# Seven quarter products instead of eight in the gated products of the experts' second parts

## The chip, the core and the metric

The kernel runs on one core of a Trainium2 chip. The metric is the device time of one execution in microseconds (us): lower is better. The core has a matrix engine (TensorE, PE in the profile, with its weight loads shown apart as PEld), a vector engine (VectorE, DVE), an activation engine (ScalarE, ACT), GpSimd (POOL) and SyncE (SP), which here issues most of the loads. Matrix products write to PSUM, from where VectorE and ScalarE read them; everything else lies in SBUF. All data is 32-bit floating point. One matrix product of the kernel appears in the profile as two TensorE instructions.

## The reference, cut to what matters

Eight sequences of 256 tokens with 512 features pass through two layers. Each layer adds a recurrent attention over a context and then a feed-forward network. Layer 0's network is dense. Layer 1's is a mixture of eight experts: every token goes to two of them, and the outputs are weighted by the gate. One expert computes, with its own three matrices,

```
g = x @ w1.T          # tokens x 1024
l = x @ w3.T          # tokens x 1024
t = g * sigmoid(g) * l
y = t @ w2.T          # tokens x 512
out[token] += weight[token] * y
```

The change touches the two products `g` and `l` alone, and how the three matrices lie in SBUF.

## The kernel before

Until about 908 us the kernel runs the attention of both layers, layer 0's network and the dispatch, which writes every token's features, its index and its gate weight into its two experts' queues in DRAM, and it computes the first parts of experts 6 and 7. Then it works off the other parts. An expert's queue is computed in two **parts** (`PARTS`): the first 256 places and the following 336. The first part always runs. The second stands in a branch (`tc.If(needed > 0)`, line 736) and runs if the queue is longer than the first part. Longer queues still would be handled by `overflow` (line 865), which has a branch of its own and nothing to do in the measured data.

The order of parts is 6_1, 7_1, 0_0, 0_1, 1_0, 1_1 and so on to 5_1, where 0_1 is expert 0's second part. The loop at lines 891 to 905 issues, for each part: the load of the next expert's weights (`load_expert`, `fill_expert`, `fill_w13`), the reading of the branch's condition on TensorE, ScalarE and VectorE, and the part (`part`, `expert_part`). Beside the part runs a background generator `bg`, one step of it after each hidden chunk: `prepare` (line 652) loads the tokens of coming parts (`r`, line 671) and turns them with TensorE transposes (`turn`, lines 643 to 648; `rt` in the profile), so that features lie on partitions.

In `compute` the 1024 hidden features of an expert are eight chunks `k` of 128. `hidden` multiplies, for chunk k, the four 128x128 blocks of `w1` with the tokens into the PSUM tile `gp`, and those of `w3` into `lp`. In a first part both fit in one PSUM bank (`gl`, 2 x 256 columns). ScalarE takes the tanh of half of `gp` (line 548), VectorE multiplies it out (lines 549, 550), and `add` (line 703) accumulates `y` for two or three blocks of 128 tokens over all chunks. The y products of chunk k are issued behind the gated products of chunk k+1. PSUM has three banks for `gp`/`lp`/`gl` and three for `y`. At a part's end `weigh` (line 725) multiplies by the gate weight and adds to the old rows that `old_rows` gathered (GpSimd, line 679), and `new_rows` scatters them (line 687). In the last part, 5_1, the y products of all chunks stand at the end, block by block, so that each block can leave while the next is multiplied.

A tile scheduler sets the order of instructions on each engine and the waits; where `manual_schedule` is named, the program's own order holds for an engine. A tile pool has a fixed number of buffers, and a new tile waits for the last reader of the tile whose buffer it takes. The weights have a pool of two buffers of 48 KB per partition (`wts`); the tokens and most activations are in `v4` (11 buffers of 4 KB), and token rows, old rows and small tiles are in `u2` (16 buffers).

Of the kernel before, what the change touches and what calls it, by code (L numbers as in the profile page):

```python
# [17 lines left out]
P = 128  # L18
# [32 lines left out]
def flamingo_kernel(  # L51
# [20 lines left out]
    nc = tc.nc  # L72

    const = ctx.enter_context(tc.tile_pool(name="const", bufs=1))
    wts = ctx.enter_context(tc.tile_pool(name="wts", bufs=2))
    work = ctx.enter_context(tc.tile_pool(name="work", bufs=2))
    small = ctx.enter_context(tc.tile_pool(name="small", bufs=2))
    dram = ctx.enter_context(tc.tile_pool(name="dram", bufs=1, space=DRAM))
# [1 line left out]
    ps_o = ctx.enter_context(tc.tile_pool(name="ps_o", bufs=3, space=PSUM))  # L80
    ps_st = ctx.enter_context(tc.tile_pool(name="ps_st", bufs=2, space=PSUM))

    def v4(name):
        return work.tile([P, DC, T], FP, tag="v4", name=name, bufs=11)

    def u2(shape, name):
        return work.tile(shape, FP, tag="u2", name=name, bufs=16)
# [25 lines left out]
    def load_first():  # L113
# [4 lines left out]
            nc.sync.dma_start(out=t[:, :, bs], in_=ctx_in[:, :, bs])  # L118
        return t

    def new_w13(name):
        return tuple(wts.tile([P, DC, HH], FP, tag=t, name=f"{t}_{name}") for t in ("w1", "w3"))

    def fill_w13(tiles, *srcs):
        for t, src in zip(tiles, srcs):
            nc.sync.dma_start(out=t, in_=src.rearrange("(c p) h -> p c h", p=P))
        return tiles

    def load_const(src, shape, name):
        t = const.tile(shape, FP, tag=name, name=name)  # L130
# [2 lines left out]

    first_ctx = load_first()

    w2h = [wts.tile([P, KC, D], FP, tag="w2", name=f"w2_{n}") for n in "ab"]
    turned = dram.tile([H0, D], FP, name="turned")

    def by_kj(ap, i):
        return ap.rearrange("(k j i) d -> i k j d", j=8, i=16)[i]  # L140

    for i in range(16):
        nc.sync.dma_start(out=w2h[i // KC][:, i % KC, :], in_=by_kj(W2T, i))
    wcol = [load_const(w0, [P, DC], "w0c"), load_const(td1, [P, DC], "w1c")]
    ucol = [load_const(u0, [P, DC], "u0c"), load_const(tf1, [P, DC], "u1c")]
    tgx = load_const(g_xattn.partition_broadcast(P), [P, 2], "tgx")
# [34 lines left out]
    nc.vector.memset(taken, 0.0)  # L181


    empty = constant([P, 1, ROW], "empty")
    nc.gpsimd.memset(empty[:, :, :D], 0.0)
    nc.gpsimd.memset(empty[:, :, D:], NOBODY)

# [200 lines left out]


    def transform(mat, i, scale):  # L390
        w = w2h[i // KC][:, i % KC, :]
        ps = ps_o.tile([P, D], FP, tag="o", name=f"fw_{i}")
        nc.tensor.matmul(ps, lhsT=mat, rhs=w, start=True, stop=True)
        nc.scalar.activation(w, ps, AF.Copy, scale=scale)

    def fwht_kj():
        for i in range(16):
            transform(hadm, i, 1.0)
            if i % 4 == 3:
                lo = i - 3  # L400
                for m in range(lo, i + 1):
                    nc.sync.dma_start(out=by_kj(turned, m), in_=w2h[m // KC][:, m % KC, :])
            yield

    latest_load = [None]

    def fwht_i():
        for h in range(2):
            latest_load[0] = nc.sync.dma_start(
                out=w2h[h], in_=turned[h * HH : (h + 1) * HH, :].rearrange("(k p) d -> p k d", p=P)  # L410
            )
        yield
        for k in range(16):
            transform(had16, k, 0.5 / H0 ** 0.5)
            yield
# [114 lines left out]
    latest = [None]  # L530

    def hidden(xn, w1, w3, k, width, name, t=None, both=None):
        cols = slice(k * P, (k + 1) * P)
        if both is not None:
            gp, lp = both[:, 0, :], both[:, 1, :]
        elif 2 * width <= 512:
            both = ps_gl.tile([P, 2, width], FP, tag="gl", name=f"gl_{name}")
            gp, lp = both[:, 0, :], both[:, 1, :]
        else:
            gp = ps_gl.tile([P, width], FP, tag="gl", name=f"gp_{name}")  # L540
            lp = ps_gl.tile([P, width], FP, tag="gl", name=f"lp_{name}")
        for ps, w in ((gp, w1), (lp, w3)):
            for c in range(DC):
                latest[0] = nc.tensor.matmul(ps, lhsT=w[:, c, cols], rhs=xn(c)[:, :width], start=(c == 0), stop=(c == DC - 1))  # L544

        if t is None:
            t = h1(width, f"t_{name}")
        nc.scalar.activation(t, gp, AF.Tanh, scale=0.5)  # L548
        nc.vector.scalar_tensor_tensor(t, t, 1.0, gp, ALU.add, ALU.mult)  # L549
        nc.vector.tensor_tensor(t, t, lp, ALU.mult)  # L550
        return t
# [51 lines left out]
    def ffn_out(s, hs, bg, n):  # L603
        for c in range(DC):
            o = ps_o.tile([P, T], FP, tag="o", name=f"o_f{s}_{c}")
            for k in range(2 * KC):
                nc.tensor.matmul(  # L607
                    o, lhsT=w2h[k // KC][:, k % KC, c * P : (c + 1) * P], rhs=hs[k],
                    start=(k == 0), stop=(k == 2 * KC - 1),
                )  # L610
                if k % 4 == 3:
                    run(bg, n)
            nc.vector.scalar_tensor_tensor(
                x[s][:, c, :], o, tgf[:, 0:1], x[s][:, c, :], ALU.mult, ALU.add
            )
# [2 lines left out]
    experts = {}  # L618

    def new_expert(name):  # L620
        return (*new_w13(name), wts.tile([P, KC, D], FP, tag="w2", name=f"w2_{name}"))

    def fill_expert(tiles, e):
        fill_w13(tiles, w1T[e], w3T[e])
        nc.sync.dma_start(out=tiles[2], in_=w2T[e].rearrange("(k p) d -> p k d", p=P))
        return tiles

    def load_expert(e):
# [18 lines left out]
        for dst, cs in dsts:  # L647
            nc.scalar.copy(dst, tp[:, cs, :rows])

    parts, metas = {}, {}  # L650

    def prepare(e, i):
        lo, width = PARTS[i]
        name = f"{e}_{i}"
        n = -(-width // P)
        mt = small.tile([P, n, 4], FP, tag="mt", name=f"mt_{name}", bufs=9)
        r0 = e * NT + lo
        nc.sync.dma_start(out=mt, in_=queue[r0 : r0 + n * P, D:ROW].rearrange("(b p) d -> p b d", p=P))
        metas[name] = unpack(e, mt, n, f"e{name}")
        per = DC if DC * width <= DC * T else 2  # L660
        tiles = [v4(f"q_{name}_{j}") for j in range(DC // per)]
        views = [
            t.rearrange("p c t -> p (c t)")[:, : per * width].rearrange("p (c t) -> p c t", c=per)
            for t in tiles
        ]
        yield
        for b in range(n):
            rows = min(P, width - b * P)
            bs = slice(b * P, b * P + rows)
            r = u2([P, D], f"r_{name}_{b}")  # L670
            nc.sync.dma_start(out=r[:rows, :], in_=queue[r0 + b * P : r0 + b * P + rows, :D])
            dsts = [(v[:, :, bs], slice(j * per, (j + 1) * per)) for j, v in enumerate(views)]
            turn(r, dsts, f"{name}_{b}", rows)
            yield
        parts[name] = lambda c: views[c // per][:, c % per, :]

    def old_rows(who, b, end, name):
        g = u2([P, D], f"g_{name}")
# [17 lines left out]
    def compute(weights, xq, wt, g, width, name, bg=iter(()), n=0, leave=None):  # L696
        w1, w3, w2 = weights
        blocks = [(b, min(P, width - b * P)) for b in range(len(g))]
        ys = [ps_o.tile([P, D], FP, tag="o", name=f"y_{name}_{b}") for b, _ in blocks]
        ts = []  # L700

        def add(k, b, rows):
            nc.tensor.matmul(  # L703
                ys[b][:rows, :], lhsT=ts[k][:, b * P : b * P + rows], rhs=w2[:, k, :],
                start=(k == 0), stop=(k == KC - 1),
            )

        for k in range(KC):
            ts.append(hidden(xq, w1, w3, k, width, f"{name}_{k}"))
            if k > 0 and leave is None:  # L710
                for block in blocks:
                    add(k - 1, *block)
            run(bg, n)
        for b, rows in blocks:
            for k in range(KC - 1 if leave is None else 0, KC):
                add(k, b, rows)
            if leave is not None:
                weigh(g[b], ys[b], wt, b, rows)
                leave(b)
        if leave is None:  # L720
            for b, rows in blocks:
                weigh(g[b], ys[b], wt, b, rows)

    def weigh(g, y, wt, b, rows):
        nc.vector.scalar_tensor_tensor(  # L725
            g[:rows, :], y[:rows, :], wt[:rows, b : b + 1], g[:rows, :], ALU.mult, ALU.add
        )

    def expert_part(weights, xq, meta, width, name, bg, n, end=NT, needed=None, last=False):
        who, wt = meta  # L730
        blocks = range(-(-width // P))
        g = [old_rows(who, b, end, f"{name}_{b}") for b in blocks]
        if needed is None:
            compute(weights, xq, wt, g, width, name, bg, n)
        else:
            with tc.If(needed > 0):  # L736
                compute(
                    weights, xq, wt, g, width, name, leave=(lambda b: new_rows(who, b, g[b], end)) if last else None
                )
        if not last:  # L740
            for b in blocks:
                new_rows(who, b, g[b], end)
# [55 lines left out]

    def part(e, i, bg, n, end=NT, needed=None, last=False):
        name = f"{e}_{i}"  # L800
        expert_part(experts[e], parts[name], metas[name], PARTS[i][1], name, bg, n, end, needed, last)

    bg = chain(wkv(1, NS - 1), dispatch(NS - 1))
    for e in EARLY:
# [86 lines left out]
    for at, (e, i) in enumerate(todo):  # L891
# [9 lines left out]
            engines = busy + [mybir.EngineType.Pool] * (at == len(todo) - 1)  # L901
            needed = nc.values_load(needs[0:1, e : e + 1], engines=engines, min_val=0, max_val=1)  # L902
        bg = prepare_on(at)
        part(e, i, bg, 1, NT, needed, at == len(todo) - 1)
        take(bg)


# [44 lines left out]
```

## Time and profile before

| | us |
|---|---|
| median of three runs | 1601.11 (1598.48 to 1602.63) |
| the profiled execution, its own time | 1602.78 |
| its span in the trace | 1601.1 |
| mean granted TensorE clock | 0.986 |
| TensorE busy, 913 to 1600 us | 664.6 of 687 |
| VectorE busy, 913 to 1600 us | 126.1 |
| ScalarE busy, 913 to 1600 us | 61.1 |
| mean DMA share, 913 to 1600 us | 0.25 |

A group line of the profile reads: line, engine, operation, output <- inputs with buffer numbers left out, size of the weight block, output shape, count | busy time and mean duration in ns | idle time ahead of it on its engine and what ended it. A timeline line reads: start, duration of the whole run of like instructions, engine, line, operation, count, and idle time before it in brackets. TensorE's instructions overlap, so the distance between two starts is the cost of one, not its duration. `gp`, `lp` are a second part's products, `gl` a first part's, `gl_f` layer 0's, `y` the output products of the experts.

One expert takes about 100.3 us of TensorE from the start of one first part (1188.63) to the next (1288.9): some 43.5 us for the first part and 56.8 for the second.

### The profile page before, as it was taken

The page shows a single profiled execution, that of the slowest core. Times are in us where ns is not written, and L with a number is a line of the kernel's source. Part 1 is how long each engine was busy: PE and PEld are TensorE (multiplying, and loading weights), DVE is VectorE, ACT ScalarE, POOL GpSimd, SP SyncE. Part 2 cuts the span into 40 slices and gives each one's busy share as a digit, 9 for nine tenths or more (in the row PEclk, how much of TensorE's full clock was granted, in tenths as well). Part 3 has the DMA queues.
Part 4 walks back from the last instruction along what each step waited for, and adds up shares of the span by engine and source line. Part 5 has one row for each costly group of instructions (what it writes and reads, how often), then busy time and mean ns, then how long its engine had stood idle before and what let it go on. Part 6 is the DMA issues. An engine that isn't in the chain of part 4 may idle for free. (4 is left out here: it accounts for less than half of the span.)

```text
span 1601.1 us, 16764 instructions
## 1 busy us (share of the span) xinstructions
PE 1524.4 (95%) x6496; PEld 1149.8 (72%) x6496; DVE 762.6 (48%) x1779; ACT 270.6 (17%) x641; POOL 143.7 (9%) x190
## 2 busy tenths in 40 slices
PE   5999999999999999999999899899999999999996
PEld 2978788787888878888787655476667576675763
DVE  6582886868788687887337212122112121121221
ACT  5140222122121221222111100011001010010100
POOL 1000001010000101001101201012101011010110
PEclk9999999999999999999999999999999999999998
DMA  9950000010100101001441305146041050420000
GB/s 350 358 177 14 27 27 27 27 54 27 38 29 14 54 14 47 21 14 72 182 181 47 95 0 189 69 151 214 30 175 56 17 219 27 172 73 13 26 30 17
DMA packets 67802, 134.97 MB, mean 84 GB/s; under 512 B 11644, under 2 KB 25084, under 8 KB 67712
## 3 DMA queue, kind: packets, MB, share of 16 engines
q1 hardware_dynamic: 57600, 108.44, 18.7%
q0 software_dynamic: 8960, 25.25, 4.5%
q8 instruction: 55, 0.90, 0.2%
q14 instruction: 35, 0.29, 0.1%
q10 hardware_dynamic: 1152, 0.09, 0.0%
HBM read 100.05 MB, written 37.90 MB: 86 GB/s over the span
## 5 line engine op out<-in xcount | busy, mean ns | idle before, releaser
L703 PE MATMUL y<-w_e,t 128*128 128x512 f32 (+1 forms) x592 | 270.4, 592 | 0.0
L544 PE MATMUL gl<-q,w_e 128*128 128x256 f32 x1024 | 236.8, 384 | 8.7 <-DVEq L868 6.8
L544 PE MATMUL gl_f<-xn,w_b 128*128 128x256 f32 (+1 forms) x1152 | 236.0, 361 | 1.6 <-DVE t_f L550 1.6
L544 PEld LDWEIGHTS gl<-q,w_e 128*128 128x128 f32 x1024 | 194.9, 193 | 52.3 <-issue 28.2
L544 PE MATMUL gl_f<-xn,w_a 128*128 128x256 f32 (+1 forms) x1152 | 230.9, 359 | 1.0 <-DVE xn L272 0.9
L544 PEld LDWEIGHTS gl_f<-xn,w_b 128*128 128x128 f32 x1152 | 202.9, 193 | 29.4 <-issue 2.6
L544 PEld LDWEIGHTS gl_f<-xn,w_a 128*128 128x128 f32 x1152 | 200.2, 193 | 24.0 <-DVE xn L272 1.2
L703 PEld LDWEIGHTS y<-w_e,t 128*128 128x128 f32 (+1 forms) x592 | 107.8, 182 | 107.5 <-issue 93.2
L544 PE MATMUL gp<-q,w_e 128*128 128x336 f32 x448 | 137.5, 451 | 2.5 <-issue 2.5
L544 PE MATMUL lp<-q,w_e 128*128 128x336 f32 x448 | 135.7, 446 | 0.0
L549 DVE SCALAR_TENSOR_TENSOR t<-t,gp 128x336 f32<-128x336 f32 x56 | 28.2, 504 | 220.9 <-ACT t L548 220.9
L549 DVE SCALAR_TENSOR_TENSOR t<-t,gl 128x256 f32<-128x256 f32 x64 | 26.7, 418 | 222.9 <-ACT t L548 222.9
L544 PEld LDWEIGHTS gp<-q,w_e 128*128 128x128 f32 x448 | 85.9, 192 | 58.5 <-issue 25.2
L607 PE MATMUL o_f<-t_f,w_b 128*128 128x256 f32 x512 | 123.5, 383 | 2.3 <-DVE t_f L550 2.3
L607 PE MATMUL o_f<-t_f,w_a 128*128 128x256 f32 x512 | 123.7, 382 | 0.0
L544 PEld LDWEIGHTS lp<-q,w_e 128*128 128x128 f32 x448 | 85.1, 190 | 41.6 <-issue 0.2
L303 DVE RECIPROCAL e<-e 128x512 f32<-128x512 f32 (+1 forms) x34 | 107.4, 3158 | 0.0
L607 PEld LDWEIGHTS o_f<-t_f,w_a 128*128 128x128 f32 x512 | 97.2, 191 | 13.4 <-issue 0.5
L607 PEld LDWEIGHTS o_f<-t_f,w_b 128*128 128x128 f32 x512 | 94.2, 190 | 15.9 <-DVE t_f L550 4.7
L548 ACT ACTIVATE t_f<-gl_f 128x256 f32<-128x256 f32 (+1 forms) x144 | 50.1, 355 | 264.8 <-PE gl_f L544 264.0
L687 POOL DMA_INDIRECT out<-g,who_e x40 | 40.3, 1006 | 595.6 <-DVE g L725 460.6
L548 ACT ACTIVATE t<-gp 128x336 f32<-128x336 f32 x56 | 25.3, 451 | 334.0 <-PE gp L544 334.0
(182 smaller groups left out, 1215.9 us busy)
## 6 DMA issues: line engine op xcount, KB each, us to landing
w_e<-in_w1T SPq DMA_DIRECT2D x8, 2048.0 KB
w_e<-in_w3T SPq DMA_DIRECT2D x8, 2048.0 KB
w_e<-in_w2T SPq DMA_DIRECT2D x8, 2048.0 KB
queue<-empty SPq DMA_DIRECT2D x8, 1290.0 KB
r<-queue SPq DMA_DIRECT2D x32, 256.0 KB
c<-in_ctxT SPq DMA_DIRECT2D x15, 512.0 KB
out<-xr SPq DMA_DIRECT2D x16, 256.0 KB
x<-in_xT SPq DMA_DIRECT2D x7, 512.0 KB
```

The costliest lines, as they stand in the source:

```text
L303: nc.vector.reciprocal(den, den)
L544: latest[0] = nc.tensor.matmul(ps, lhsT=w[:, c, cols], rhs=xn(c)[:, :width], start=(c == 0), stop=(c == DC - 1))
L548: nc.scalar.activation(t, gp, AF.Tanh, scale=0.5)
L549: nc.vector.scalar_tensor_tensor(t, t, 1.0, gp, ALU.add, ALU.mult)
L607: nc.tensor.matmul(o, lhsT=w2h[k // KC][:, k % KC, c * P : (c + 1) * P], rhs=hs[k], start=(k == 0), stop=(k == 2 * KC - 1),)
L687: nc.gpsimd.indirect_dma_start(out=out[:end, :], out_offset=bass.IndirectOffsetOnAxis(ap=who[:, b : b + 1], axis=0), in_=g, in_offset=None ...
L703: nc.tensor.matmul(ys[b][:rows, :], lhsT=ts[k][:, b * P : b * P + rows], rhs=w2[:, k, :], start=(k == 0), stop=(k == KC - 1),)
```

## The change

In a second part of 336 tokens each of the two gated products, a matrix of 1024 x 512 times one of 512 x 336, is divided once in each of its three dimensions: the weights into four quarters of 512 hidden features by 256 input features, the tokens into four quarters of 256 features by 168 tokens. Plain multiplication has eight quarter products. The changed kernel forms seven (Strassen's scheme in Winograd's form), of sums of the quarters, and combines the seven results by additions. One step `k` now gives the hidden chunks k and k+4 together, so there are four steps instead of eight.

- **Weights as quarter tiles.** `w1` and `w3` of an expert are four tiles each, `w2` is four tiles, all of 0.5 MB. Each has a transfer of its own: twelve per expert instead of three. They lie in the pool of the activations, which grows from 11 to 35 buffers of the same size; the weights' own pool is gone.
- **Sums of the weights** (`sum_weights`): for each of `w1` and `w3` three new tiles, and a fourth sum written over quarter `a21` (`last_sum`) once nothing reads `a21` any more. They are made on VectorE in the background of the expert's first part, the last ones right ahead of the second part's branch. **Sums of the tokens** (`sum_tokens`): four operations on VectorE.
- For expert 7, whose first part lies before the loop, both are issued just ahead of the branch of 6_1. For expert 6 no sums are made: 6_1 keeps `compute`.
- **`compute_paired`** replaces `compute` in the other seven second parts. In a step, for each of the two matrices: three products of two matmuls each into the tile `pa`, three into `pb`, and the seventh products of both matrices into one tile `pc`. ScalarE copies one product, VectorE adds the others in four operations and, for `pc`, one more; then follow one tanh and two VectorE operations over 672 columns. The y products of a step are issued among the products of the next (`late`, `put`). TensorE's order in it is written out by hand (`manual_schedule`).
- In a first part the background now takes two steps after each chunk instead of one. The tile `empty` moves to the pool `u2`, and the hidden tiles of second parts as well.

```diff
     def fill_w13(tiles, *srcs):
-        for t, src in zip(tiles, srcs):
-            nc.sync.dma_start(out=t, in_=src.rearrange("(c p) h -> p c h", p=P))
+        for j in range(2):
+            for t, src in zip(tiles, srcs):
+                for i in range(2):
+                    nc.sync.dma_start(
+                        out=t[i][j],
+                        in_=src[i * 2 * P : (i + 1) * 2 * P, j * D : (j + 1) * D].rearrange("(c p) h -> p c h", p=P),
+                    )
...
+    HALF = PARTS[1][1] // 2
+
+    def sum_weights(e, last=False):
+        sums[e] = []
+        for n, w in zip("13", experts[e]):
+            (a11, a21), (a12, a22) = w
+            s1, s2, s4 = (v4(f"s{i}_{n}_{e}", (P, 2, D)) for i in (1, 2, 4))
+            sums[e].append((a11, a12, a22, s1, s2, a21, s4))
+            nc.vector.tensor_tensor(s1, a21, a22, ALU.add)
+            yield
+            nc.vector.tensor_tensor(s2, s1, a11, ALU.subtract)
+            yield
+            nc.vector.tensor_tensor(s4, a12, s2, ALU.subtract)
+            yield
+        if last:
+            last_sum(e)
+
+    def last_sum(e):
+        for a11, *_, s3, _ in sums[e]:
+            nc.vector.tensor_tensor(s3, a11, s3, ALU.subtract)
+
+    def sum_tokens(name):
...
+        nc.vector.tensor_tensor(t1, b12, b11, ALU.subtract)
+        nc.vector.tensor_tensor(t2, b22, t1, ALU.subtract)
+        nc.vector.tensor_tensor(t3, b22, b12, ALU.subtract)
+        nc.vector.tensor_tensor(t4, b21, t2, ALU.subtract)
...
+        def product(ps, to, k, weights, toks):
+            for c in range(2):
+                nc.tensor.matmul(
+                    ps[:, to, :], lhsT=weights[:, c, k * P : (k + 1) * P], rhs=toks[:, c, :],
+                    start=(c == 0), stop=(c == 1),
+                )
+
+        def six(k, n):
+            a11, a12, a22, s1, s2, s3, s4 = sums[e][n]
+            r = u2([P, 4, HALF], f"h{n}_{name}_{k}")
+            ps = ps_gl.tile([P, 3, HALF], FP, tag="gl", name=f"pa{n}_{name}_{k}")
+            product(ps, 0, k, a11, b11)
+            product(ps, 1, k, a12, b21)
+            product(ps, 2, k, s2, t2)
+            nc.scalar.copy(r[:, 1, :], ps[:, 0, :])
+            nc.vector.tensor_tensor(r[:, 0:4:3, :], ps[:, 1:3, :], twice(r[:, 1:2, :]), ALU.add)
+            yield
+            ps = ps_gl.tile([P, 3, HALF], FP, tag="gl", name=f"pb{n}_{name}_{k}")
+            product(ps, 0, k, s1, t1)
+            product(ps, 1, k, s3, t3)
+            product(ps, 2, k, s4, b22)
+            nc.vector.tensor_tensor(r[:, 1:3, :], ps[:, 0:2, :], twice(r[:, 3:4, :]), ALU.add)
+            nc.vector.tensor_tensor(r[:, 3, :], ps[:, 1, :], r[:, 1, :], ALU.add)
+            nc.vector.tensor_tensor(r[:, 1, :], ps[:, 2, :], r[:, 1, :], ALU.add)
+            yield r
...
+        for k in range(KC // 2):
+            last = k == KC // 2 - 1
+            rs = []
+            for n in range(2):
+                both = six(k, n)
+                next(both)
+                put(2 * n if not last else 0)
+                rs.append(next(both))
+            put(2 if not last else 0)
+            ps = ps_gl.tile([P, 2, HALF], FP, tag="gl", name=f"pc_{name}_{k}")
+            for n in range(2):
+                product(ps, n, k, sums[e][n][2], t4)
+            put(len(late))
+            for n in range(2):
+                nc.vector.tensor_tensor(rs[n][:, 2, :], ps[:, n, :], rs[n][:, 2, :], ALU.add)
+            t = u2([P, 4, HALF], f"t_{name}_{k}")
+            nc.scalar.activation(t, rs[0], AF.Tanh, scale=0.5)
+            nc.vector.scalar_tensor_tensor(rs[0], t, 1.0, rs[0], ALU.add, ALU.mult)
+            nc.vector.tensor_tensor(rs[1], rs[0], rs[1], ALU.mult)
...
+            if leave is None:
+                late += [(j, b, rows) for j in (k, k + 4) for b, rows in blocks]
+        put(len(late))
+        for b, rows in blocks:
+            if leave is not None:
+                for i in range(KC):
+                    add(i // 2 + i % 2 * 4, b, rows)
+            weigh(g[b], ys[b], wt, b, rows)
...
     def expert_part(weights, xq, meta, width, name, bg, n, end=NT, needed=None, last=False):
...
+            paired = weights in sums
+            if paired and weights not in EARLY:
+                last_sum(weights)
...
             with tc.If(needed > 0):
-                compute(
-                    weights, xq, wt, g, width, name, leave=(lambda b: new_rows(who, b, g[b], end)) if last else None
-                )
+                if paired:
+                    with tc.manual_schedule(engines={mybir.EngineType.PE}):
+                        compute_paired(weights, sums[name], wt, g, name, done)
+                else:
+                    compute(experts[weights], xq, wt, g, width, name, leave=done)
...
         bg = prepare_on(at)
-        part(e, i, bg, 1, NT, needed, at == len(todo) - 1)
+        if i == 0:
+            bg = chain(bg, sum_tokens(f"{e}_1"), sum_weights(e))
+        elif e == EARLY[0]:
+
+            take(chain(sum_weights(EARLY[1], True), sum_tokens(f"{EARLY[1]}_1")))
+        part(e, i, bg, 2, NT, needed, at == len(todo) - 1)
         take(bg)
```

## The prediction

> **What bounds the kernel now.** I read the busy shares first, then the groups by line, then the timeline of TensorE in one expert, then the list of TensorE's waits after 913 us.
>
> ```profile
> PE 1524.4 (95%) x6496; PEld 1149.8 (72%) x6496; DVE 762.6 (48%) x1779; ACT 270.6 (17%) x641; POOL 143.7 (9%) x190
> ...
> PEclk9999999999999999999999999999999999999998
> ...
> L544 PE MATMUL gp<-q,w_e 128*128 128x336 f32 x448 | 137.5, 451 | 2.5 <-issue 2.5
> L544 PE MATMUL lp<-q,w_e 128*128 128x336 f32 x448 | 135.7, 446 | 0.0
> L549 DVE SCALAR_TENSOR_TENSOR t<-t,gp 128x336 f32<-128x336 f32 x56 | 28.2, 504 | 220.9 <-ACT t L548 220.9
> ```
>
> TensorE is busy 95% of the span at nearly full clock, and VectorE waits 220.9 us for work ahead of line 549: the bound is TensorE. The change touches the experts' second parts, the groups with 336 columns. They have 448 + 448 hardware instructions, 128 to a part, so **seven** second parts run, not eight. Which one is skipped stands in the timeline:
>
> ```profile
> 1081.04 3.60 PE L703 MATMUL y<-w_e,t 128*128 128x512 f32 x8
> 1086.53 8.83 PE L544 MATMUL gl<-q,w_e 128*128 128x256 f32 x32 [1.89 <-DVEq L736]
> ...
> 1128.43 3.60 PE L703 MATMUL y<-w_e,t 128*128 128x512 f32 x8
> 1131.87 2.42 PE L544 MATMUL gp<-q,w_e 128*128 128x336 f32 x8
> 1134.13 2.42 PE L544 MATMUL lp<-q,w_e 128*128 128x336 f32 x8
> 1136.39 2.42 PE L544 MATMUL gp<-q,w_e 128*128 128x336 f32 x8
> 1138.65 2.42 PE L544 MATMUL lp<-q,w_e 128*128 128x336 f32 x8
> 1140.91 2.74 PE L703 MATMUL y<-w_e,t 128*128 128x512 f32 x6
> ```
>
> Expert 0's first part ends at 1084.6 and expert 1's first part (`gl`) follows at once, with no `gp` between: 0_1 does not run. Part 6_1 keeps the old form. So six parts are paired at run time: 7_1, 1_1, 2_1, 3_1, 4_1, 5_1. Starts 2.26 us apart for 8 instructions give a **pitch** of 282.5 ns per 336-column instruction (the mean of 446 to 451 counts overlapping ends).
>
> **The gain on TensorE.** A second part has 8 chunks x 2 matrices x 4 matmuls x 2 instructions = 128, at 282.5 ns: 36.16 us. After, 4 steps x 2 matrices x 7 products x 2 matmuls x 2 instructions = 224 of 168 columns. No row has 168 columns. Pitches beside it: 512 columns 430 ns (6 in 2.58 us), 336 columns 282.5, 256 columns 215.6 (16 in 3.45 us, next start at 1052.97 after 1049.52), and 128 columns:
>
> ```profile
> 61.41 7.53 PE L544 MATMUL gl_f<-xn,w_b 128*128 128x128 f32 x66
> 68.78 1.39 PE L544 MATMUL gl_f<-xn,w_a 128*128 128x128 f32 x11
> ```
>
> that is 7.37 us / 66 = 111.7 ns (115 in two other stretches). A line through the long ones is 2.5 + 0.833 per column: 142.5 ns for 168; the 128-column rows lie 2 to 6 ns above that line. I take 144: 224 x 144 = 32.26 us, 3.90 us saved in a part, **23.4 us in six** (142.5 gives 25.4; 148 gives 18.1). The y products and first parts keep their instructions, and up to 908 us TensorE, VectorE and ScalarE keep theirs in order.
>
> **A rule that speaks against it.** The shorter instruction still needs its own 128-column weight load, and there are 224 loads instead of 128. The Trainium skill, "TensorE: Matmul & The Clock Gate", says in "LDWEIGHTS (loading the stationary operand)" that a load takes columns / 1.2 ns, 107 for 128, and in Part 3 ("The mechanism") that a load overlaps a running matmul only where the row group differs; here all rows are used. By that rule a part would go from 128 x (282.5 + 107) = 49.9 us to 224 x (142.5 + 107) = 55.9: 6 us slower, 36 in all. The row above decides against it: 66 instructions of 128 columns, each with its own load (68 loads in that window), keep 111.7 ns, and the loads' 193 ns mean is more than the pitch, so loads overlap matmuls there.
>
> **VectorE and ScalarE inside a paired part.** Rows: 128 columns 280 ns, 256 410, 336 504, 512 684, 1024 1221; between them 168 is 321 and 672 is 852. ScalarE: 160 columns 311, 512 about 600, 1024 1057; tanh of 672 about 750. Per step VectorE does 2 x (504 + 504 + 321 + 321) + 2 x 321 + 2 x 852 = 5.65 us. TensorE has 56 x 144 = 8.06, and 12 y instructions x 430 = 5.16 from the second step on: 13.2. VectorE hides. Three PSUM banks give TensorE three groups (5.1 us) ahead of an eviction. The chain behind a step's last product is 2 x 321 + 750 + 852 + 852 = 3.1 us; the next step's first groups, and at the end 6 of the last y's, 5.16 us, cover it. The last part, 5_1, sums each block of y on its own at its end, but six of a block's eight products need only earlier steps: 12 x 0.43 = 5.2 us, again more than 3.1. I put +0.5 for it (0 to 1).
>
> **The sums.** Six sums of weights (6 x 1.22 = 7.3 us) and four of tokens (2 us) lie in the first part's background. VectorE is 18% busy after 913, and the first part lasts 43.5 us: no cost, since four sums in a row (4.9 us) fit a step of 5.17. The last two (2.44 us) stand ahead of the branch and read tiles that the eighth chunk still uses: they end some 3.9 us after its start, its y's are wanted at 5.17. +0.2 for each of five experts, 1.0 (0 to 2).
>
> **Once, at 6_1.** Expert 7's sums have no first part to lie in: 8 x 1.22 + 4 x 0.50 = 11.8 us stand on VectorE ahead of its branch into 6_1, behind the transposes that end near 913.9.
>
> ```profile
> 916.41 4.21 PE L544 MATMUL gp<-q,w_e 128*128 128x336 f32 x8 [2.54 <-issue]
> 920.46 2.42 PE L544 MATMUL lp<-q,w_e 128*128 128x336 f32 x8
> 922.72 2.42 PE L544 MATMUL gp<-q,w_e 128*128 128x336 f32 x8
> ```
>
> Before, VectorE came into it at 921.14, early enough. After, it enters near 926.5 and frees the first bank near 927.5, while TensorE has filled three banks at 924.98 (or 922.7, if one bank is still held): idle 2.5 to 5 us. An idle stretch costs a second time: after 2.54 us the first eight instructions took 4.05 us instead of 2.26; after 1.89 us (1086.5) the granted clock was 0.80 over 8.7 us, +1.9. So +4.5 (2 to 7). VectorE's small overflow operations (16 or 17 x 0.2 us), done before 914.2 until now, partly move behind 6_1: +1 at 7_1 (0 to 3).
>
> **Loads.** SP issues twelve transfers of 0.5 MB per expert instead of three of 2 MB. The bytes are equal; at the start rows of 2 KB (W2, 7 to 14 us) moved at 341 GB/s and rows of 4 KB (24 to 32 us) at 410. SP goes in order, and more of the twelve now wait for the second part's last readers: three of the next expert's quarters can come early, nine (4.5 MB) and behind them the token rows `r` (1.2 MB) after the part. Before, w1 was issued at 1181.41 and `r` at 1189.36, when some 2.9 of the 6 MB had landed at 370 GB/s (1182 to 1203). Now 5.7 MB take 15.4 us at 370, 16.7 at 341, while the transposes of `r` stand some 16 us into the first part, and VectorE's token sums behind them. Where `r` comes late, TensorE idles: +0.5 in each of four experts, 2 (0 to 8). The quarters of the weights are wanted in the order in which they are loaded.
>
> **Sum.** 1602.8 (profiled run; span 1601.1 and 1.7 outside) - 23.4 + 0.5 + 1.0 + 4.5 + 1.0 + 2 = 1588.4. The median shown is 1601.1, 1.7 under that run: **1587**. The bounds: 1578 (142.5 ns, low ends) to 1604 (148 ns, all high ends at once); together they will hardly all be high, so this case alone is 1578 to 1597.
>
> **Rivals.**
> 1. *Evictions set the pace* (slower side). A step's evictions cross two engines: VectorE waits in order for ScalarE's copy and tanh, and PSUM has three banks. If TensorE must wait for the 3.1 us chain without cover, a part loses up to 4 x 3.1 = 12.4 us. It decides from 3.9 / 4 = 0.98 us of wait per step. For it: VectorE has 22 operations in a part now and 52 after. Against it: 5.65 of 13.2 us. At 1.5 us per step: 1587 + 36 = 1623. Chance 0.09.
> 2. *Weight loads set the pace* (slower side): at the loads' mean of 193 ns, 224 x 193 = 43.2 us against 36.2: 42 us more than before, about 1650; break-even at 161 ns. Against it the 111.7 ns. Chance 0.04.
> 3. *The loads come late*: a stall of 2 us in each of five first parts, paid twice for the clock, is 20 us, less the 2 counted: 1605. For it: one queue in order, at the full DMA share of 1.0 in 1182 to 1203. Against it: quarters come in the order of use. Chance 0.09.
> 4. *The stalls vanish*: the transposes for expert 7 end earlier or TensorE's queue hides 6_1; 1579. Chance 0.14, inside the range.
>
> The forecast itself has 0.64. Within 0.3% (4.8 us) is what a measurement of this kernel cannot tell from no change. Faster: forecast and rival 4, plus a fifth of rivals 1 and 3, less the forecast's upper tail: 0.83. Same: 0.06, half of rival 3 and the tail. Slower: 0.11. The range 1576 to 1602 leaves out rivals 1 and 2, half of 3 and a little below.
>
> **What would show it.** A pitch of 142 to 148 ns in the 168-column rows (right) or above 161 (rival 2); TensorE idle in a paired part with VectorE as releaser (rival 1); idle of 2 to 5 us near 925 released by VectorE, with a low clock behind it; idle ahead of the transposes or of `gl` released by DMA (rival 3); a part from its first product to the next expert's `gl` of 52.9 us instead of 56.8. The prediction falls if six paired parts do not each shorten by 3 to 4.3 us, or if more than 10 us are lost between parts.

## The result and the profile after

The changed kernel takes 1587.72 us (median of four, 1586.59 to 1588.75) against 1601.41 before: a ratio of 0.9917, 95% interval 0.9900 to 0.9934. In a later series both were a little slower, 1590.45 and 1604.21, with the same ratio of 0.9919 (0.9905 to 0.9932). The profiled execution took 1587.68 us, its span 1585.9, so 15.2 us less of span than before (1601.1). The prediction said 1587.

The page of the changed kernel, busy shares, clock, and the new products:

```profile
PE 1500.9 (95%) x7072; PEld 1196.0 (75%) x7072; DVE 923.1 (58%) x2055; ACT 281.8 (18%) x665; POOL 149.3 (9%) x190
...
PEclk8999999999999999999999999999999999999998
...
L807 PE MATMUL pa<-q,w_e 128*128 128x168 f32 x384 | 62.6, 306 | 0.0
```

TensorE is still the bound, with 576 more instructions and 23.5 us less busy time; VectorE is busy 160.5 us more, and nearly all of that is hidden. The count of 384 for `pa` with quarters of the weights is 64 for each of six parts: six paired parts ran, as read from the profile before.

The timeline of TensorE in the changed kernel, the beginning of part 1_1 and its end:

```profile
1128.71 1.30 PE L807 MATMUL pa<-q,w_e 128*128 128x168 f32 x8
1129.85 0.73 PE L807 MATMUL pa<-ta,s 128*128 128x168 f32 x4
1130.42 0.73 PE L807 MATMUL pb<-ta,s 128*128 128x168 f32 x4
...
1170.92 10.46 PE L798 MATMUL y<-w_e,h 128*128 128x512 f32 x24
1181.22 7.07 PE L568 MATMUL gl<-q,w_e 128*128 128x256 f32 x32
```

Eight instructions start 1.14 us apart, four 0.57: the pitch is 142.5 ns. The part lasts 1128.71 to 1181.22, 52.51 us, where the same part took 56.76 before. TensorE never waits in it. That is 4.25 us a part, 25.5 in six. The span fell by 15.2, so **10.3 us were lost elsewhere**. The list of what TensorE waited for, from 900 us on, after and (below it) in a fence of its own before:

```profile
PE rt L670 <- DMA r<-queue: 7.4, 7, 2.9
PE gl L568 <- DVEq L1024: 6.0, 1, 6.0
PE gl L568 <- DVE wt_e L663: 2.7, 1, 2.7
PE gp L568 <- issue: 2.6, 1, 2.6
```

```profile
PE gl L544 <- DVEq L868: 6.8, 1, 6.8
PE gp L544 <- issue: 2.5, 1, 2.5
PE gl L544 <- DVEq L736: 1.9, 1, 1.9
```

The columns are the time in all, how often, and the longest. The first line is new: the transposes `rt` wait seven times for token rows `r` from DRAM. The other three have their counterparts before. Taking the starts of the parts from both timelines gives the whole account:

| stretch | before | after | difference |
|---|---|---|---|
| up to 6_1 | 916.41 | 915.78 | -0.63 |
| 6_1 (plain in both) | 58.55 | 59.60 | +1.05 |
| 7_1 and the overflow branch | 63.68 | 58.95 | -4.73 |
| 0_0 | 47.89 | 47.94 | +0.05 |
| 1_0 | 45.34 | 46.44 | +1.10 |
| 1_1 | 56.76 | 52.51 | -4.25 |
| 2_0 | 43.52 | 48.38 | +4.86 |
| 2_1 | 56.76 | 52.51 | -4.25 |
| 3_0 and 3_1 | 100.28 | 98.35 | -1.93 |
| 4_0 and 4_1 | 100.28 | 97.98 | -2.30 |
| 5_0 | 42.56 | 42.64 | +0.08 |
| 5_1 up to its y products' end, and the tail | 69.07 | 64.82 | -4.25 |

With 4.25 us taken out for each paired part, 1_0 lost 1.10, 2_0 4.86, 3_0 2.32 and 4_0 1.95: 10.2 us, nearly the whole loss. How one of them goes wrong is in SP's timeline, before (first fence) and after (second), around the end of 1_1:

```profile
1181.41 0.38 SPq L126 DMA_DIRECT2D w_e<-in_w1T  x1
1183.67 0.38 SPq L126 DMA_DIRECT2D w_e<-in_w3T  x1
1188.82 0.37 SPq L625 DMA_DIRECT2D w_e<-in_w2T  x1
1189.36 5.08 SPq L671 DMA_DIRECT2D r<-queue  x5
```

```profile
1181.84 1.03 SPq L136 DMA_DIRECT2D w_e<-in_w1T  x2
1182.92 1.52 SPq L136 DMA_DIRECT2D w_e<-in_w3T  x2
1184.54 2.35 SPq L144 DMA_DIRECT2D w_e<-in_w2T  x4
1187.51 8.17 SPq L695 DMA_DIRECT2D r<-queue  x5
```

Before, 2_0 begins at 1188.63 and two thirds of the weights have been on their way for up to 7 us; the five `r` are issued 0.7 to 5.3 us after the part's start. After, 2_0 begins at 1181.22, eight quarters (and a ninth at 1181.42) are issued behind that point. The first of the five `r` leaves SP at 1187.51, 6.3 us into the part, and takes 13.1 us to land, at 1200.6; the last leaves SP at 1195.4. TensorE came to its transposes at 1197.8 and began them at 1200.67:

```profile
1195.02 2.75 PE L568 MATMUL gl<-q,w_e 128*128 128x256 f32 x12
1200.67 1.76 PE L670 MATMUL rt<-ident,r 128*128 128x128 f32 x8 [2.90 <-DMA r<-queue]
```

The 2.90 us of idle time cost 4.86: from 1199 to 1206 the granted clock was 0.76, and the eight transposes took 1.76 us where a run of eight takes 0.94 to 1.07 in the profile before. The other waits for `r` cost little more than themselves: 4.5 us of waits in 1_0, 3_0 and 4_0 stand for 5.4 us of loss, and the clock behind the 1.77 us of 3_0 and the 1.33 us of 4_0 stayed at 1.00.

There is a second half to the wait in 2_0. Before, the first transpose of that part stands here:

```profile
1208.02 0.60 PE L646 MATMUL rt<-ident,r 128*128 128x128 f32 x4
```

That is 19.4 us into the part. The changed kernel comes to it after 16.6 us, and the rows land after 19.4. At the old place in TensorE's order they would hardly have been late; no run tested that.

### The profile page after: what moved, and what is told of

Read it like the earlier page. It is cut to its first block, busy times and chain, and to the rows that moved or that the text cites. A ratio compares the mean times of both kernels' runs of the same rounds, so it can differ in the third digit from the quotient of the medians.

```text
span 1585.9 us, 18555 instructions
## 1 busy us (share of the span) xinstructions
PE 1500.9 (95%) x7072; PEld 1196.0 (75%) x7072; DVE 923.1 (58%) x2055; ACT 281.8 (18%) x665; POOL 149.3 (9%) x190
## 5 line engine op out<-in xcount | busy, mean ns | idle before, releaser
L728 PE MATMUL y<-w_e,t 128*128 128x512 f32 (+1 forms) x304 | 141.1, 593 | 0.0
L798 PE MATMUL y<-w_e,h 128*128 128x512 f32 (+1 forms) x288 | 129.5, 592 | 0.0
L728 PEld LDWEIGHTS y<-w_e,t 128*128 128x128 f32 (+1 forms) x304 | 56.5, 188 | 46.8 <-issue 39.1
L798 PEld LDWEIGHTS y<-w_e,h 128*128 128x128 f32 (+1 forms) x288 | 49.6, 177 | 54.5 <-issue 54.5
L573 DVE SCALAR_TENSOR_TENSOR t_f<-t_f,gl_f 128x256 f32<-128x256 f32 (+1 forms) x144 | 54.2, 383 | 48.3 <-ACT t_f L572 48.2
L572 ACT ACTIVATE t<-gl 128x256 f32<-128x256 f32 x64 | 24.6, 384 | 312.3 <-PE gl L568 312.3
L807 PEld LDWEIGHTS pa<-q,w_e 128*128 128x128 f32 x384 | 57.8, 190 | 8.1 <-issue 7.8
L807 PE MATMUL pa<-q,w_e 128*128 128x168 f32 x384 | 62.6, 306 | 0.0
```

The source lines that it names most:

```text
L728: nc.tensor.matmul(ys[b][:rows, :], lhsT=ts[k][:, b * P : b * P + rows], rhs=w2_of(w2, k), start=(k == 0), stop=(k == KC - 1),)
L798: nc.tensor.matmul(ys[b][:rows, :], lhsT=ts[k][:, b * P : b * P + rows], rhs=w2_of(w2, k), start=(k == 0), stop=(k == KC - 1),)
L807: nc.tensor.matmul(ps[:, to, :], lhsT=weights[:, c, k * P : (k + 1) * P], rhs=toks[:, c, :], start=(c == 0), stop=(c == 1),)
```

## The experiments

**Token rows ahead of the weights.** In the changed kernel SP takes the rows behind the quarters. Here the rows' transfers are issued by the loop, ahead of `load_expert`; `prepare` finds them ready.

```diff
         if nxt < NE and order[nxt] not in experts:
+            if i == 0 and at > 2:
+                for e_, i_ in todo[at + 1 : at + 3]:
+                    for b in range(-(-PARTS[i_][1] // P)):
+                        rows_of[e_, i_, b] = load_rows(e_, i_, b)
             load_expert(order[nxt])
...
-            r = u2([P, D], f"r_{name}_{b}")
-            nc.sync.dma_start(out=r[:rows, :], in_=queue[r0 + b * P : r0 + b * P + rows, :D])
+            r = rows_of.pop((e, i, b), None)
+            if r is None:
+                r = load_rows(e, i, b)
```

> The changed kernel with one move: the five transfers of token rows r that stand behind an expert's twelve weight quarters on SP are issued ahead of the quarters that have to wait for the second part's last readers. Theory A (the rows stand behind nine quarters that wait, and TensorE waits for the rows; the four first parts 1_0, 2_0, 3_0 and 4_0 lost 1.1, 4.9, 2.3 and 1.9 us): no wait of TensorE for r is left, and the time falls by about 10 us from 1587.7, to 1576 to 1580. Rival B (the rows come late because the many small transfers share the bandwidth, whatever their order): the waits for r stay, 1585 to 1589.

1578.04 us (five runs, 1576.04 to 1581.03), ratio to before 0.9852 (0.9830 to 0.9874), below the changed kernel's interval. The list of waits has no line for `r` any more, and SP's timeline shows the rows issued ahead of the quarters that have to wait, three of the five well before the next expert begins at 1279.58 and two right behind that point:

```profile
1267.20 13.39 SPq L683 DMA_DIRECT2D r<-queue  x5
1280.63 1.04 SPq L136 DMA_DIRECT2D w_e<-in_w3T  x2
1281.71 1.20 SPq L136 DMA_DIRECT2D w_e<-in_w1T  x2
```

Theory A is right, and this kernel beats both others: the same transfers in another order give back the 10 us. From one second part to the next (1131.14 to 1227.06) an expert takes 95.92 us here, 4.36 less than the 100.28 before. That is the 4.25 of the pairing and a little more, so nothing is left of the loss, and the sums in the first part cost nothing.

**Plain products, everything else as changed.** It tells whether the smaller transfers alone make the rows late.

```diff
-                if paired:
+                if False:
                     with tc.manual_schedule(engines={mybir.EngineType.PE}):
                         compute_paired(weights, sums[name], wt, g, name, done)
```

> The changed kernel with its quarter tiles, its twelve transfers and all sums on VectorE, but every second part computed with the eight plain products of before. One quarter of w1 and of w3 has been overwritten by a sum there, so this run's second parts use sums in place of those quarters. Theory A: what is lost comes from the loads and not from the seven products, so the waits for r stay at 5 to 9 us in all and the time is 1587.7 plus six times 4.25, about 1613 (1608 to 1616). Rival B (the paired parts hold buffers of the small pool longer and so delay the rows): the waits for r go, and the time is near that of before, 1600 to 1605.

1602.39 us (twelve runs, 1599.57 to 1606.97), ratio to before 1.0004 (0.9991 to 1.0016). I expected 1613 by theory A; it **fell**, and the time is that of rival B. Quarter tiles, twelve transfers and the sums together cost nothing that shows. One wait for `r` is left, 1.6 us in 1_0. SP's timeline of this run shows what differs:

```profile
1187.69 1.43 SPq L144 DMA_DIRECT2D w_e<-in_w2T  x3
1189.17 2.78 SPq L695 DMA_DIRECT2D r<-queue  x5
1192.36 12.80 SPq L136 DMA_DIRECT2D w_e<-in_w1T  x2
1206.03 0.88 SPq L136 DMA_DIRECT2D w_e<-in_w3T  x2
```

Only three transfers of `w2`, not nine quarters, stand ahead of `r` at a part's end; `w1` and `w3` of the following expert leave during the first part. Twelve transfers in SP's order are not the cause by themselves. In the plain run TensorE never reads the six sums of weights, so a buffer that holds one comes free as soon as VectorE has done with it. What SP waited for while it loaded expert 4's weights agrees. In the changed kernel it was, most of all, the y products of the paired part 2_1 (first fence); in the plain run `w1` and `w3` waited for products of the first part (16.7 us) and for VectorE's sums (second fence), and had all left by 1228.2.

```profile
SPq L136 <- PE y L798: 54.9, 2, 33.3
```

```profile
SPq L136 <- DVE s L763: 11.1, 1, 11.1
```

A step with seven products reads every quarter of the weights, where a plain chunk reads the first half of them for four chunks and then the second. So the rival was right that the pairing holds buffers; it named the wrong pool, since these are the large buffers of the weights. Which buffer each quarter takes over is not in the profile and is not shown.

**Half the columns.** Each product is done as two of 84 columns.

```diff
-            for c in range(2):
-                nc.tensor.matmul(
-                    ps[:, to, :], lhsT=weights[:, c, k * P : (k + 1) * P], rhs=toks[:, c, :],
-                    start=(c == 0), stop=(c == 1),
-                )
+            for cs in (slice(0, HALF // 2), slice(HALF // 2, HALF)):
+                for c in range(2):
+                    nc.tensor.matmul(
+                        ps[:, to, cs], lhsT=weights[:, c, k * P : (k + 1) * P], rhs=toks[:, c, cs],
+                        start=(c == 0), stop=(c == 1),
+                    )
```

> The changed kernel with every product of 168 columns done as two of 84, so 448 instructions and weight loads in a paired part instead of 224. Theory A (the streaming sets the pitch, loads lie beside it): 2.5 + 0.833 x 84 = 72.5 ns, 32.5 us instead of 31.9 in a part, the time rises by 3 to 5 us to about 1591. Rival B (a weight load of 128 columns has a floor of about 107 ns that the pitch cannot go below): 448 x 107 = 47.9 us in a part, 16 more, the time is about 1684 (1670 to 1695).

1697.64 us (four runs, 1695.61 to 1699.24): rival B, a little above its range. The timeline of TensorE in it, with the columns as above:

```profile
1150.56 1.06 PE L808 MATMUL pa<-ta,s 128*128 128x84 f32 x8
1151.45 1.06 PE L808 MATMUL pb<-ta,s 128*128 128x84 f32 x8
1152.35 1.06 PE L808 MATMUL pb<-tb,w_e 128*128 128x84 f32 x8
```

Eight starts lie 0.89 us apart: 111 to 112 ns an instruction, not 72.5. By that pitch a part has 448 x 111.6 = 50.0 us of gated products instead of 31.9, 18.1 more; six times that is 108.6, and the run is 109.9 us above the changed kernel. The same 111.7 ns stand in the 128-column rows that the prediction used. So **a product's instruction with its own full weight load has a floor of about 111.6 ns**, and 128 columns already lie on it. 168 columns stay above it by 31 ns.

It is no floor of every instruction. In 5_0 of the kernel before, four transposes of 80 tokens stand ahead of a run of products:

```profile
1509.31 0.44 PE L646 MATMUL rt<-ident,r 80*128 80x80 f32 x4
1509.59 3.66 PE L544 MATMUL gl<-q,w_e 128*128 128x256 f32 x16
```

They start 70 ns apart, near the 69 that 2.5 + 0.833 x 80 gives, each with a load of 128 columns of its own. The profile shows these loads with 140 ns, those of products with 190. That speaks for the load as what sets the floor of products, but no run shows it apart.

**More work for VectorE.** Two, then five, further operations of 672 columns in each step, whose results nobody reads (shown for two).

```diff
             nc.vector.scalar_tensor_tensor(rs[0], t, 1.0, rs[0], ALU.add, ALU.mult)
+            for _ in range(2):
+                nc.vector.tensor_tensor(t, rs[0], rs[0], ALU.add)
             nc.vector.tensor_tensor(rs[1], rs[0], rs[1], ALU.mult)
```

> The changed kernel with two further VectorE operations over 672 columns in each step of a paired part, between the two last ones: 1.7 us longer from a step's last product to its hidden values (3.1 to 4.8 us), and 7.4 us of VectorE in a step. Theory A (evictions are well covered by the y products and the next products): no change, 1586.5 to 1589. Rival B (evictions are at the edge of setting the pace): up to 1.7 us in each of 24 steps, 1600 to 1628.

> The changed kernel with five further VectorE operations over 672 columns in each step of a paired part, 4.3 us: 7.4 us from a step's last product to its hidden values and 9.9 us of VectorE in a step of 13.2. Theory: now the chain is longer than the 5.2 us of y products that cover it at a part's end, so TensorE waits some 2 us at the end of each part and 1 to 2 us at some steps: 20 to 45 us slower than the control, with waits for VectorE inside the paired parts. Rival (TensorE has enough other work at hand): within 5 us of the control.

With two, 1594.21 us (six runs, 1590.38 to 1598.94), between the two expectations, above the changed kernel's first four runs but in a series in which the kernel before also spread from 1595.53 to 1606.97. The profile has no wait of TensorE in the paired parts (part 1_1: 1130.58 to 1183.10, 52.52 us), but 9.5 us of waits for `r` instead of 7.4. What set the rest apart stays open. With five, 1591.91 (five runs, 1590.79 to 1599.23) against a control of 1590.45 in the same series; waits for VectorE inside the paired parts are 2.0 us in all. My theory of 20 to 45 us was wrong, and the timeline of VectorE says why (`L861` is an added operation, `L862` the last product of the chain):

```profile
1151.61 0.86 DVE L861 TENSOR_TENSOR t<-h 128x672 f32<-128x672 f32 x1
1152.38 0.85 DVE L862 TENSOR_TENSOR h<-h,h 128x672 f32<-128x672 f32 x1
1153.15 0.85 DVE L861 TENSOR_TENSOR t<-h 128x672 f32<-128x672 f32 x1
```

The scheduler put most of the added operations behind that last product, so the load grew and the chain hardly did. It shows that VectorE has room for 4.3 us more in a step.

**A longer chain.** So that the operations cannot be moved, each now works in place on the hidden values (shown for two).

```diff
             nc.vector.scalar_tensor_tensor(rs[0], t, 1.0, rs[0], ALU.add, ALU.mult)
+            for _ in range(2):
+                nc.vector.tensor_tensor(rs[0], rs[0], rs[0], ALU.max)
             nc.vector.tensor_tensor(rs[1], rs[0], rs[1], ALU.mult)
```

> The changed kernel with two further VectorE operations over 672 columns in each step of a paired part that each read the result of the one before and stand ahead of the last product, so that they cannot be put behind it: the chain from a step's last product to its hidden values grows from 3.1 to 4.8 us. Theory (5.2 us of y products cover the chain at a part's end): no wait of TensorE for VectorE in the paired parts, a part of 52.5 us. Rival (the cover is shorter than counted): waits of up to 1.7 us per part or step.

> The same with five such operations: the chain is 7.4 us. Theory: 7.4 less 5.2, so TensorE waits about 2.2 us at each part's end ahead of its last y products, and at some steps for a bank; a part of 55 to 60 us. Rival (other work can always be put in): a part stays at 52.5 us.

One run of each: 1593.52 and 1656.10 us, before 1605.28. The lists of waits, of the run with two and of the run with five:

```profile
PE y L798 <- DVE h L862: 1.7, 5, 0.4
```

```profile
PE y L798 <- DVE h L862: 40.8, 16, 4.0
```

With two, TensorE is idle for 0.35 us at five places, each time at the first y product of a part, behind the second step's products. The end of the chain and that product in part 1_1, of the changed kernel and then of the run with two (lines of two engines; `L860` and `L862` are the same operation):

```profile
1139.35 0.85 DVE L860 TENSOR_TENSOR h<-h,h 128x672 f32<-128x672 f32 x1
1141.82 1.88 PE L798 MATMUL y<-w_e,h 128*128 128x512 f32 x4
```

```profile
1143.09 0.85 DVE L862 TENSOR_TENSOR h<-h,h 128x672 f32<-128x672 f32 x1
1143.99 1.98 PE L798 MATMUL y<-w_e,h 128*128 128x512 f32 x4 [0.35 <-DVE h L862]
```

In the changed kernel the chain ends at 1140.20, **1.6 us ahead of the product** that needs it: that is what it has to spare at its tightest place. With two more operations it ends 2.1 us later in the part, since another operation of VectorE slips in between, and the product starts 0.5 us later. The part takes 53.1 us and not 52.5: the rival was right, by little.

With five, the waits are 40.8 us and part 1_1 takes 64.3 us, more than the 55 to 60 expected. The theory held in kind: TensorE waits for the chain. But the longest waits stand where it did not look, at the first y product of a part (3.59 us in 1_1) more than at the end (2.48). And TensorE's busy time in 1_1 is 56.9 us instead of 52.5, at a granted clock of 0.95.

**Without the sums ahead of 6_1.** Part 7_1 is computed plainly, five parts are paired. The control is the changed kernel in the same series.

```diff
-        elif e == EARLY[0]:
-
-            take(chain(sum_weights(EARLY[1], True), sum_tokens(f"{EARLY[1]}_1")))
```

> The changed kernel without the sums ahead of 6_1, so part 7_1 is computed plainly and five parts are paired. The prediction's sum put 5.5 us of loss on those sums (4.5 at 6_1 and 1 at 7_1) against 4.25 gained: by it this run would be about 1 us faster than the control, or the same. The trace of the changed kernel shows no TensorE wait for those sums: by it the run is slower than the control by 3 to 5 us.

> The changed kernel itself, as a control for the others of this call, since the run with two more VectorE operations came out some 6 us higher while its paired parts kept their 52.5 us. If that was the drift of the earlier runs: about 1590 to 1594 here too, when the kernel before is at 1602 to 1603. If the added operations cost it: 1586 to 1589.

1592.99 us (1588.15 to 1594.98) against 1590.45 (1589.18 to 1592.27): ratios of 0.9933 (0.9920 to 0.9947) and 0.9919 (0.9905 to 0.9932), which overlap. The sign speaks for the trace, the size (2.5 us) doesn't settle it. TensorE has no idle time for the sums. But 6_1 takes 58.54 us in this run, 59.41 in the control and 59.60 in the first profile, so one would say that they cost 0.9 to 1.1 us. The other profiles say otherwise. The sums stand ahead of 6_1 in seven more of the runs above, and there 6_1 takes 58.54 or 58.55 us, as in the kernel before. The 5 us from the first product of 6_1, of the control, of the run with five more operations (which has the sums as well) and of this run (columns: window, its length, busy time of TensorE, weight loads, VectorE, ScalarE, GpSimd, then granted clock, DMA share, GB/s):

```profile
916.96:921.96 5.00, 5.00 (x9) 3.20 (x10) 5.00 (x6) 0.00 (x0) 3.87 (x3) 0.50 0.36 105
```

```profile
918.15:923.15 5.00, 5.00 (x12) 3.18 (x13) 5.00 (x6) 0.45 (x1) 3.89 (x3) 0.66 0.34 105
```

```profile
915.07:920.07 5.00, 5.00 (x12) 3.17 (x13) 0.51 (x1) 0.45 (x1) 1.98 (x2) 0.66 0.38 110
```

With VectorE full of sums the granted clock is 0.50 in one and 0.66 in the other; with VectorE nearly idle it is 0.66. So **the sums do not hold the clock down**, and no cost of them shows. In the two profiles of the changed kernel the clock had begun to fall ahead of 6_1's first product (0.87 and 0.83 over the 5 us before it; 1.00 in the nine others). Why it did so in these two stays open.

The control also bears on the two added operations of before: its 1590.45 lies where drift was expected (1590 to 1594), so a part of the 6.5 us by which that run was slower is drift.

## Why the prediction was right

The total was right (1587 for 1587.72) and the mechanism too: seven products of shorter instructions save TensorE 4 us a part, VectorE hides the sums and evictions, and losses between the parts take back two fifths. But the terms were off in both directions, and that the total came so close is luck. By its own sign of being wrong, more than 10 us lost between the parts, the prediction stands on the edge: 10.3 were lost.

- **Six paired parts, 0_1 skipped:** right.
- **Pitch of a 168-column instruction:** 144 ns predicted, 142.5 measured; 25.5 us saved instead of 23.4. I read the 128-column rows' 2 to 6 ns above the line as a price of short instructions that would partly hold at 168. They lie on the floor of 111.6 ns, which does not touch 168.
- **The rule on weight loads** (the Trainium skill, "TensorE: Matmul & The Clock Gate", "LDWEIGHTS (loading the stationary operand)", 107 ns for 128 columns): its size is about the floor measured with 84 columns, 111.6 ns. Added to the matmul, as Part 3's condition on row groups would have it, it would have meant, as an estimate, 55.9 us a part; the 224 products took 224 x 142.5 = 31.9. The measurement decides: here loads overlap matmuls of the same rows, and the longer of the two, columns or floor, counts. The prediction's reading of the row was right in outcome. But the row could not show that the loads were free, only that they were not more than 111.7 ns.
- **VectorE and ScalarE in the paired part:** no wait, as predicted. The cover of 5.16 us that I counted at the part's end was not the tightest place: that is the first y product, with 1.6 us to spare.
- **The sums in the first parts (+1.0) and the last part (+0.5):** no cost is seen; 5_0 took 0.08 us more and 5_1 with its tail was 4.25 shorter like the others.
- **6_1 (+4.5) and 7_1 (+1):** over-sized. 6_1 lost 1.05 us, by the clock alone and not by the sums. The step that failed is that VectorE would enter near 926.5: two instructions of 128x1024 start 1.13 us apart, the row's mean of 1.22 counts an overlap; the sums began at 912.35, were done at 923.2, and the branch took no time that shows. 7_1 has one gap of 0.2 us, and the overflow branch behind it was 0.8 us shorter.
- **The loads (+2, range 0 to 8):** the term that was mis-sized most, 10.2 us, beyond its range. The place was right (rows behind nine quarters, transposes some 16 us into the part). I counted the bytes at 370 GB/s, 15.4 us, and 0.5 us for each lateness: by that, all rows are there at about 1197 in 2_0. The first of them landed at 1200.6. From 1182 to 1203 the DMA moved 338 GB/s, and 7.1 MB went through, with the next quarter and the old and new rows among them, where I had counted 5.7. And the longest wait was paid again in the clock (2.90 us of wait, 4.86 of loss). Rival 3, which put this at 20 us, had the mechanism, at twice the size.

The errors nearly cancel: 4.9 us too much at 6_1 and 7_1, 1.4 too much at the sums in the first parts and the last part, 8.2 too little at the loads, 2.1 of gain too little at the pitch; and the stretch up to 6_1 was 0.6 shorter by itself. In sum, predicted losses of 9.0 stand against 10.3 measured, a predicted gain of 23.4 against 25.5.

## What to carry to other kernels

A scheme that trades columns for fewer multiplications gains as long as the instruction stays above the floor that its weight load seems to set; measure that floor with a product of half the columns before cutting further (worked out from these runs, a second level of the scheme would have 224 x 2 x 7/8 = 392 instructions of 84 columns in a part, 43.7 us at 111.6 ns instead of 31.9). When a change makes each step read all of its operands, count which buffers now come free only at the end and what queues behind the transfers that wait for them: here a small transfer behind nine large ones cost 10 of 25 us, and a change of order gave it back. To measure the slack of a chain, lengthen it with operations that depend on each other; independent ones are moved out of it.

## What the runs showed of the hardware that was not expected

- A TensorE instruction of a product with its own full weight load does not go below 111.6 ns: 84 and 128 columns have the same pitch, 168 columns follow 2.5 + 0.833 per column. Transposes of 80 columns do go below, to 70 ns.
- Weight loads overlap matmuls on the same rows: 142.5 ns a pair at 168 columns, on the line of the longer instructions, where a load is shown with a mean of 190 ns.
- Idle time of TensorE of 2.5 us ahead of 6_1 left a granted clock of 0.66 over the next 5 us in nine profiles and 0.50 in two, whether VectorE was full or nearly idle beside it. After 2.9 us in 2_0 it was 0.76 over 7 us, which cost nearly another 2 us; after 1.8 and 1.3 us it stayed at 1.00.
